# A four-layer graph network on one core: softmax transposes, the first quad's edge sums and the order of the first iteration are changed

## The chip, the cores and the metric

One core of one Trainium2 chip runs the whole network in one launch. The metric is device time in microseconds (us). TensorE (PE in the profile, PEld for its weight loads) multiplies, VectorE (DVE) and ScalarE (ACT) work on tiles, GpSimd (POOL) issues indirect transfers and some elementwise work, and SyncE (SP) issues plain transfers.

## The reference

Input x holds 128 batches of 128 nodes with 256 features, in fp32. Each of four layers computes `x = layernorm(x + g(x))`. The first g is graph attention over 512 edges with four heads:

```python
Xq = (H @ W_lin.T).reshape(bt, n, h, dh);  Xv = (H @ W_val.T).reshape(bt, n, h, dh)
e = einsum('behd,hd->beh', leaky_relu(Xq[:, src] + Xq[:, dst], 0.2), a)
e = e + log(A0[src, dst] + 1e-8)
attn = softmax of e over the edges that share src
Y = segment_sum(attn * Xv[:, dst], src) @ W_out.T
```

The second g is three graph convolutions with weighting adj*adj and widths 512, 1024 and 256, with relu after the first two. The third multiplies with the diagonal, upper and lower parts of adj and three weights, and adds a bias. The fourth normalises adj, applies it, and runs two linear layers, each with a batch norm over all batches and nodes.

## The kernel before, in words

The batches are worked on in 32 quads of four. A quad goes through these steps, each a function:

- `values_in` (L237, L239) transposes x; `values` (L251 to L253) makes the queries `qt` and the values `xv` of the first quads with one product per batch. Later quads use `queries`, a Strassen-like scheme of seven products (class `Seven`: p1, p5, p2, p6, p7, p4, p3; S1 to S4 are sums of the left blocks, `sums_a`, L180 to L183). `spill` (L260) writes the queries to DRAM.
- `gather` and `gather_last` (L329, on POOL's queue) fetch for 128 edges at a time the query rows of src and add those of dst. The edges are sorted by src; `perm` is the permutation as a 0/1 matrix, and `sorted_columns` (L998) makes the sorted index columns by products with it. An edge list of 512 has NE = 4 chunks, and a quad R = 16 rows (four batches, four heads).
- `score` (L344 to L349) computes e for one chunk, in `es`; the last chunk adds the log weights.
- `softmax_parts` is a generator, so that the caller decides where each part stands: four transposes of 128x16 to 16x128 (L356), a running maximum forward (L358) and backward (L361), subtract (L364), Exp (L365), a running sum forward (L367) and a running maximum backward (L369).
- `attention` (L379 to L383) transposes numerator and denominator back in eight pieces of 16x128 and divides; `scatter` (L389 on POOL, then L392 on SP) writes the attention into a dense matrix in DRAM and loads it; `by_row` (L402) reorders it.
- `aggregate` (L416) applies it to the values, `stage_a` (L430, L433, norms L105 to L120) ends layer 1.
- Layer 2: `mix1` (L441), `first` (L455) or `first_seven` (L280), `mix2` (L498), `late_sums` (L509, L510), `second` (L535, fourteen block products, with callbacks `between[i]` after product i), `third` (L616, a generator that yields after each quarter), `third_mix` (L629), `third_norm` (POOL's bias add is L640).
- Layer 3 is `stage_e` (L652, L657, L666; a generator). Layer 4 starts with `stage_f` (L697) and `hidden` (L726, L739), and a last phase after all quads ends it.

The order on every engine is that of the program (`manual_schedule`), and each engine runs its queue in order. In `iteration(k)` five quads are at work at once: k-1 in layers 3 and 4, k in layer 2, k+1 from aggregation to layer 2's first part, k+2 in scores and softmax, k+3 in queries and gather. `start()` sorts the edges, prepares matrices made from adj, and brings quads 0 to 3 as far as iteration 0 needs them. `iteration_0()` is written out by hand. In it, third runs whole, then aggregation and `stage_a` of quad 1, all of `stage_e(0)`, and layer 2's first part of quad 1.

In `start()` quad 0 is spilled and gathered like the others, the loads of `w1_sb` and the later weights are issued after `scatter(0)`, and quad 3's `values` stand after `stage_a(0)`.

Of the kernel before, what the change touches and what calls it, by code (L numbers as in the profile page):

```python
# [8 lines left out]
F32 = mybir.dt.float32  # L9
# [12 lines left out]
DROP = -1e30  # L22


@with_exitstack
def gnn_stack(ctx: ExitStack, tc: tile.TileContext, x, adj, w_qv_t, a, w_out_t, src, dst,
# [18 lines left out]
    P = 128  # L45
# [82 lines left out]
    with ExitStack() as phase:  # L128
        cst = phase.enter_context(tc.tile_pool(name="cst", bufs=1))

        class Quad:
            pass
# [91 lines left out]

        def temp(name):
            return wk.tile([P, 512], F32, tag="t", name=name, bufs=6)
# [15 lines left out]
        def values(k, i, copy=None, queue=None):  # L242
# [3 lines left out]
            if i == 0:  # L246
                s.qt = wk.tile([P, QB, D], F32, tag="xb", name=f"qt{k}", bufs=1)
                s.xv = ws.tile([P, QB, D], F32, tag="xv", name=f"xv{k}", bufs=3)
# [5 lines left out]
            if i == QB - 1:  # L254
                spill(k, queue)

        def spill(k, queue=None):
            s = quads[k]
            s.qd = q_dram[k % 4]
            (queue or nc.sync).dma_start(s.qd, s.qt.rearrange("p b d -> p (b d)"))  # L260
# [48 lines left out]
        def gather(k, z=None, chunks=range(NE - 1)):  # L309


            s = quads[k]
            s.z = z or {}
            for c in chunks:
                if c not in s.z:
                    s.z[c] = z_buffer(k, c)
            jobs = [(t, c) for t in range(2) for c in chunks]
            if k == 0:
                jobs = [(0, 0), (0, 1), (1, 0), (0, 2), (1, 1), (0, 3), (1, 2), (1, 3)]
            for t, c in jobs:  # L320
                gather_one(k, t, c)
# [11 lines left out]
        def gather_last(k):  # L333
            quads[k].z[NE - 1] = z_buffer(k, NE - 1)
            for t in range(2):
                gather_one(k, t, NE - 1)

        def score(k, c):

            s = quads[k]  # L340
            if c == 0:
                s.es = ws.tile([P, NE, R], F32, tag="es", name=f"es{k}", bufs=1)
# [5 lines left out]
            if c == NE - 1:  # L348
                nc.vector.tensor_add(s.es, s.es, log_col.unsqueeze(2).to_broadcast([P, NE, R]))  # L349

        def softmax_parts(k):

            s = quads[k]
            pe = ps("pe")
            for c in range(NE):
                nc.tensor.transpose(pe[:R, c * P:(c + 1) * P], s.es[:, c, :], ident)  # L356
            f = wk.tile([R, E], F32, tag="f", name="f", bufs=1)
            nc.vector.tensor_tensor_scan(f, reset_f, pe[:R, :], initial=0.0, op0=ALU.add, op1=ALU.max)  # L358
            yield
            m = wk.tile([R, E], F32, tag="m", name="m", bufs=1)  # L360
            nc.vector.tensor_tensor_scan(m[:, ::-1], reset_b[:, ::-1], f[:, ::-1], initial=0.0,  # L361
                                         op0=ALU.add, op1=ALU.max)
            yield
            nc.vector.tensor_sub(f, pe[:R, :], m)  # L364
# [4 lines left out]
            nc.vector.tensor_tensor_scan(m[:, ::-1], keep_b[:, ::-1], m[:, ::-1], initial=0.0,  # L369
                                         op0=ALU.mult, op1=ALU.max)  # L370
            s.ex, s.den = f, m

        def attention(k):

            s = quads[k]
            pa = ps("pat")[:, :2 * NE * R].rearrange("p (s c r) -> p s c r", s=2, c=NE)
            for i, t in ((0, s.ex), (1, s.den)):
                for c in range(NE):
                    nc.tensor.transpose(pa[:, i, c, :], t[:, c * P:(c + 1) * P], ident[:R, :R])  # L379
            rden = wk.tile([P, NE, R], F32, tag="rden", name="rden", bufs=1)  # L380
            nc.vector.reciprocal(rden, pa[:, 1])
            s.at = wk.tile([P, NE, R], F32, tag="at", name="at", bufs=1)
            nc.vector.tensor_mul(s.at, rden, pa[:, 0])  # L383

        def scatter(k):
            s = quads[k]
            ad = att_dram[k % 2]
            for c in range(NE):
                nc.gpsimd.indirect_dma_start(out=ad, out_offset=bass.IndirectOffsetOnAxis(ap=att_idx[:, c:c + 1], axis=0),  # L389
                                             in_=s.at[:, c, :], in_offset=None)  # L390
            s.ad = wk.tile([P, N * R], F32, tag="ad", name=f"ad{k}", bufs=1)
# [397 lines left out]
        def iteration(k):  # L789
# [6 lines left out]
            parts = quads[a].layer2 if a > 0 else iter(())  # L796
# [5 lines left out]
            for _ in parts:  # L802
                pass
            if has_c:
                between = {i: [] for i in range(14)}
                if has_e:
# [632 lines left out]
```

## Time and profile before

| what | us |
|---|---|
| runs: lowest, median, highest of 3 | 3214.33, 3216.5, 3216.66 |
| the profiled execution, by its own time | 3216.53 |
| its span, first to last instruction | 3214.8 |
| PE busy | 3132.8 (97%) |
| DVE busy | 2143.9 (67%) |
| ACT busy | 1276.8 (40%) |
| POOL busy | 663.5 (21%) |

Instructions are grouped by line, engine and operand shapes, as `out<-in`. An fp32 product appears as two matmul records, a transpose as one. Records are pipelined: a record's own duration is longer than the distance from its start to the next start, and the distance is what a product costs. PEclk is the granted share of TensorE's full clock. A line of the waits gives the engine that waited, who released it, the time in all, how often, and the longest.

### The profile page before, as it was taken

The numbers are of one execution on the slowest core, as the hardware profiler recorded it, in microseconds if no ns is written. First come the engines' busy times: TensorE is split into PE (matmuls) and PEld (weight loads), VectorE is DVE, ScalarE is ACT, GpSimd is POOL, SyncE is SP. The second block draws the span as 40 slices with busy tenths as digits, with TensorE's granted clock in tenths as the row PEclk, the third lists the DMA queues.
The fourth block names the chain that finished last, engine by engine and source line by source line (L and its number), as shares of the span: only waits on it lengthen the run. The fifth ranks groups of instructions, "written<-read, shape, count | busy, mean of one in ns | idle before, by whom it ended". The sixth has DMA issues, their size and how long they took to land. (4 is left out here: it accounts for less than half of the span.)

```text
span 3214.8 us, 41204 instructions
## 1 busy us (share of the span) xinstructions
PE 3132.8 (97%) x15884; PEld 2596.4 (81%) x15884; DVE 2143.9 (67%) x4200; ACT 1276.8 (40%) x2229; POOL 663.5 (21%) x541
## 2 busy tenths in 40 slices
PE   6999999999999999999999999999999999999997
PEld 3788888888888888888888888888888888874444
DVE  6666666666666666666666667666666666437878
ACT  2343333333333333333333333343333333326668
POOL 4202222122111111222112221111222211002135
PEclk7999999999999999999999999999999999999999
DMA  7613333333333223333333333223333321005557
GB/s 216 182 47 99 106 99 105 91 101 106 99 92 101 87 78 97 106 99 106 99 92 106 106 86 106 88 80 90 106 100 105 100 85 53 21 27 183 177 191 274
DMA packets 118756, 344.86 MB, mean 107 GB/s; under 512 B 15008, under 2 KB 51744, under 8 KB 110240
## 3 DMA queue, kind: packets, MB, share of 16 engines
q0 software_dynamic: 45552, 151.55, 19.3%
q1 hardware_dynamic: 70960, 188.71, 16.2%
q8 instruction: 126, 2.06, 0.3%
q10 hardware_dynamic: 2048, 1.97, 0.2%
q14 instruction: 70, 0.57, 0.1%
HBM read 256.20 MB, written 85.98 MB: 106 GB/s over the span
## 5 line engine op out<-in xcount | busy, mean ns | idle before, releaser
L535 PE MATMUL ph<-m,w 128*128 128x256 f32 x2048 | 464.3, 380 | 0.0
L616 PE MATMUL p<-w,h 128*128 128x256 f32 x2048 | 462.3, 379 | 0.0
L616 PEld LDWEIGHTS p<-w,h 128*128 128x128 f32 x2048 | 389.6, 190 | 65.6 <-issue 7.6
L535 PEld LDWEIGHTS ph<-m,w 128*128 128x128 f32 x2048 | 388.0, 191 | 51.0
L329 POOL DMA_INDIRECT zs<-qd,src_idx x123 | 119.5, 972 | 1390.1 <-DVE z L739 769.7
L535 PE MATMUL ph<-m,w_s 128*128 128x256 f32 x1536 | 352.5, 379 | 0.0
L666 PE MATMUL po<-l2w,ms 128*128 128x256 f32 x1536 | 348.3, 380 | 1.3 <-DVE ms L658 1.3
L535 PEld LDWEIGHTS ph<-m,w_s 128*128 128x128 f32 x1536 | 292.2, 190 | 39.3
L666 PEld LDWEIGHTS po<-l2w,ms 128*128 128x128 f32 x1536 | 285.3, 191 | 36.0 <-DVE ms L658 1.5
L329 POOL DMA_INDIRECT zs<-qd,dst_idx x123 | 211.2, 1717 | 254.9 <-DMA zs<-qd,src_idx 242.1
L112 ACT ACTIVATE ln_sd<-ln_mv,eps 128x2 f32<-128x2 f32 x192 | 56.3, 293 | 498.8 <-DVE ln_mv L107 498.8
L389 POOL DMA_INDIRECT attd<-at,att_idx x128 | 126.1, 986 | 358.9 <-DMA attd<-at,att_idx 253.5
L548 DVE TENSOR_TENSOR h<-ph,u 128x512 f32<-128x512 f32 x128 | 88.1, 689 | 167.8 <-PE ph L535 114.5
L542 ACT COPY u<-ph 128x512 f32<-128x512 f32 x128 | 74.9, 585 | 244.3 <-PE ph L535 244.3
L346 DVE TENSOR_TENSOR zs<-zs,a_bc 128x1024 f32<-128x1024 f32 x123 | 150.7, 1225 | 4.2
L347 DVE TENSOR_REDUCE es<-zs 128x16 f32<-128x1024 f32 x123 | 150.1, 1220 | 4.2
L344 DVE SCALAR_TENSOR_TENSOR zs<-zs 128x1024 f32<-128x1024 f32 x123 | 149.6, 1216 | 2.1 <-DMA zs<-qd,dst_idx 2.1
L120 DVE TENSOR_SCALAR xr<-xr,ln_mv,ln_rs 128x256 f32<-128x256 f32 x384 | 143.6, 416 | 7.0
L654 ACT COPY ms<-pm 128x512 f32<-128x512 f32 x128 | 71.1, 579 | 194.4 <-PE pm L652 191.0
L105 DVE BATCH_NORM_STATS2 ln_st<-xr 128x6 f32<-128x256 f32 x384 | 144.2, 417 | 5.5
L477 DVE TENSOR_TENSOR h<-z,adc 128x512 f32<-128x512 f32 x62 | 41.9, 675 | 153.8 <-ACT adc L471 153.8
L640 POOL TENSOR_TENSOR xb<-xr,bias 128x512 f32<-128x512 f32 x64 | 81.6, 1275 | 293.6 <-DVE xr L120 155.6
(298 smaller groups left out, 5713.1 us busy)
## 6 DMA issues: line engine op xcount, KB each, us to landing
ad<-attd SPq DMA_DIRECT2D x32, 1024.0 KB, 4.7
zd<-z SPq DMA_DIRECT2D x31, 1024.0 KB, 7.3
zl<-zd SPq DMA_DIRECT2D x62, 512.0 KB, 3.5
xr<-in_x_dram SPq DMA_DIRECT2D x32, 512.0 KB, 5.8
x3d<-xr SPq DMA_DIRECT2D x32, 512.0 KB, 2.8
x3l<-x3d SPq DMA_DIRECT2D x32, 512.0 KB, 4.9
out_dram<-x3l POOLq DMA_DIRECT2D x31, 512.0 KB, 5.3
qd<-qt SPq DMA_DIRECT2D x30, 512.0 KB, 2.6
```

Of the source, the lines that this page charges most:

```text
L105: nc.vector.bn_stats(st[:, i, :], r[:, i, :])
L120: nc.vector.tensor_scalar(r[:, i, :], r[:, i, :], mv[:, i, 0:1], rs[:, i:i + 1], op0=ALU.subtract, op1=ALU.mult)
L329: nc.gpsimd.indirect_dma_start(out=s.z[c], out_offset=None, in_=s.qd, in_offset=bass.IndirectOffsetOnAxis(ap=idx[:, c:c + 1], axis=0), com ...
L344: nc.vector.scalar_tensor_tensor(z, z, SLOPE, z, op0=ALU.mult, op1=ALU.max)
L346: nc.vector.tensor_mul(z3, z3, a_bc.unsqueeze(1).to_broadcast([P, QB, D]))
L347: nc.vector.reduce_sum(s.es[:, c, :], z.rearrange("p (r d) -> p r d", d=DH), axis=AX.X)
L389: nc.gpsimd.indirect_dma_start(out=ad, out_offset=bass.IndirectOffsetOnAxis(ap=att_idx[:, c:c + 1], axis=0), in_=s.at[:, c, :], in_offset= ...
L535: nc.tensor.matmul(bank[g][:, i].rearrange("p b n -> p (b n)"), wa[:, c, f:f + P], s.m2[:, blk_b, c].rearrange("p b n -> p (b n)"), start= ...
L548: nc.vector.tensor_add(block(g, row, col), bank[g], kept_[g])
L616: nc.tensor.matmul(p3[:, t * D:(t + 1) * D], s.h2[f // 2][:, f % 2, j + t, :], w3_sb[:, f, :], start=(f == 0), stop=(f == K2 - 1))
L640: nc.gpsimd.tensor_add(s.xb[:, j:j + 2, :], xj, bias.unsqueeze(1).to_broadcast([P, 2, D]))
L666: nc.tensor.matmul(po[:, i % 2, :], mss[i][:, t, dc, :], l2w[:, t, dc, :], start=(n3 == 0), stop=(n3 == 3 * DC - 1))
```

## The change

1. `scores` and `pair` are two new fixed tiles, set to zero once. `scores` keeps a chunk's 16 columns in a block of 32, so that one 128x128 transpose turns all four chunks; four ScalarE copies bring the blocks to `pair[:16]`. The denominator goes to `pair[32:48]`, so that `attention` transposes four pieces of 48x128 instead of eight of 16x128.
2. The parts of the softmax stand earlier in the loop: the transpose after product 11 of `second`, both maxima after product 12, the subtract ahead of `queries`, Exp after q's first product.
3. Quad 0 is neither spilled nor gathered. Its edge sums are products of a one-hot matrix (ones at src and dst) with the queries, in the order of the list; its scores take the weights in `score`, and products with `perm` sort them while they are transposed. The loads of all weights are issued before the first products. Quad 1's gathers wait for the end of this, and its dst gathers alternate with quad 0's scatters. `second_sums` and quad 3's queries stand ahead of quad 0's `by_row`.
4. `iteration_0` follows the loop's order: third's quarters lie between the steps of quads 1 and 2, and all but the first part of `stage_e(0)` goes to iteration 1's beginning. Quad 1's softmax crosses from `start` into `second(0)`.

```diff
+        scores = ctile([P, NE, GAP], "scores", pool=cst)
+        pair = ctile([GAP + R, E], "pair", pool=cst)
+        nc.vector.memset(scores, 0.0)
+        nc.vector.memset(pair, 0.0)
...
+        def ends_sum(k, h, onehot):
+            s = quads[k]
+            for c in range(NE):
+                pz = ps("pz")
+                nc.tensor.matmul(pz, onehot[:, c * P:(c + 1) * P], s.qt[:, 2 * h:2 * h + 2, :], start=True, stop=True)
+                nc.scalar.copy(s.z[c][:, h * 512:(h + 1) * 512], pz)
+        def sorted_scores(k, perm, chunks=range(NE)):
...
+            for c in chunks:
+                nc.tensor.matmul(s.pe[:R, :], s.es[:, c, :], perm[:, c, :], start=(c == 0), stop=(c == NE - 1))
...
-        def score(k, c):
+        def score(k, c, weight=None):
...
+            if weight is not None:
+                nc.vector.tensor_scalar(s.es[:, c, :], s.es[:, c, :], weight[:, c:c + 1], None, op0=ALU.add)
+            elif c == NE - 1:
...
         def softmax_parts(k):
...
-            for c in range(NE):
-                nc.tensor.transpose(pe[:R, c * P:(c + 1) * P], s.es[:, c, :], ident)
...
+            f, m = pair[:R], wk.tile([R, E], F32, tag="m", name="m", bufs=1)
+            rows = s.pe[:R, :] if s.pe is not None else None
+            if rows is None:
+                rows = f
+                pe = ps("pe")[:, :P]
+                nc.tensor.transpose(pe, scores.rearrange("p c r -> p (c r)"), ident)
+                for c in range(NE):
+                    nc.scalar.copy(f[:, c * P:(c + 1) * P], pe[c * GAP:c * GAP + R, :])
...
         def attention(k):
...
-            for i, t in ((0, s.ex), (1, s.den)):
-                for c in range(NE):
-                    nc.tensor.transpose(pa[:, i, c, :], t[:, c * P:(c + 1) * P], ident[:R, :R])
+            for c in range(NE):
+                nc.tensor.transpose(pa[:, c, :], pair[:, c * P:(c + 1) * P], ident[:GAP + R, :GAP + R])
...
+                between[11].append(lambda: next(steps, None))
+                between[12] += [lambda: next(steps, None)] * 2
...
         def iteration_0():
...
-            between[1] = [lambda: attention(1), lambda: scatter(1)]
-            between[2] = [lambda: score(2, 0), lambda: gather_last(2)]
+            between[0] = [lambda: score(2, 0), lambda: gather_last(2, range(1))]
+            between[1] = [lambda: next(quads[1].steps), lambda: next(quads[1].steps, None)]
+            between[3] = [lambda: attention(1), lambda: scatter(1), lambda: gather_last(2, range(1, 2))]
...
+            rest = third(0, 0)
+            next(rest)
+            first_seven.blocks = weight_blocks(w1_sb, w1_s)
+            for j in range(QB):
+                by_row(1, j, nc.vector.tensor_copy if j % 2 else None)
+            next(rest)
+            aggregate(1)
             score(2, NE - 1)
-            first_seven.blocks = weight_blocks(w1_sb, w1_s)
+            next(rest)
+            stage_a(1)
+            for _ in rest:
+                pass
+            steps = softmax_parts(2)
+            for _ in range(5):
+                next(steps)
+            third_mix(0, 0)
+            rest = third(0, 2)
+            next(rest)
+            third_norm(0, 0)
+            mix1(1, 0)
+            mix1(1, 2)
+            next(rest)
+            w = first_seven(1)
+            for _ in steps:
+                pass
+            run(w.p1, w.p5, w.p2)
+            next(rest)
+            attention(2)
+            scatter(2)
+            w.p6()
+            next(rest, None)
+            w.p7()
+            third_mix(0, 2)
+            w.p4()
+            w.p3()
+            third_norm(0, 2)
+            quads[0].layer2 = stage_e(0)
+            next(quads[0].layer2)
+            for i in range(QB):
+                mix2(1, i)
...
+            onehot = scratch("onehot")
...
+            for h in range(2):
+                for i in range(2):
+                    values(0, 2 * h + i, nc.scalar.copy,
+                           xv=borrowed[:, N * R:N * R + QB * D].rearrange("p (b d) -> p b d", d=D))
+                ends_sum(0, h, onehot)
...
+            sorted_scores(0, perm, range(NE - 1))
+            sorted_columns((0, 1))
+            sorted_scores(0, perm, (NE - 1,))
+            sorted_columns((2, 3))
...
+                gather_one(1, 0, c)
...
             attention(0)
...
+            scatter(0, lambda c: gather_one(1, 1, c))
```

`...` stands for what is left out.

## Prediction

> **What bounds it now.** I read the page first, for the engine that is full, and where.
>
> ```profile
> span 3214.8 us, 41204 instructions
> ...
> PE   6999999999999999999999999999999999999997
> ...
> PEclk7999999999999999999999999999999999999999
> ```
>
> TensorE is full in all but the first and last slices. The stage table, cut where layer 2's first product of each quad starts (timeline: 110.1, 201.0, 288.7, then every 87.47 us), shows where it is not:
>
> ```profile
> core 0: us, PE busy (x) PEld busy (x) DVE busy (x) ACT busy (x) POOL busy (x), PEclk, DMA share, GB/s
> 0.00:52.10 52.10, 32.91 (x120) 19.22 (x120) 30.77 (x66) 10.76 (x24) 27.92 (x28) 0.82 0.83 241
> 52.10:110.10 58.00, 43.77 (x182) 28.09 (x183) 40.13 (x64) 20.12 (x39) 14.64 (x14) 0.79 0.80 235
> 110.10:201.00 90.90, 80.01 (x399) 68.73 (x398) 55.36 (x108) 28.30 (x47) 21.33 (x18) 0.91 0.29 81
> 201.00:288.70 87.70, 87.56 (x470) 76.48 (x469) 61.20 (x113) 33.27 (x56) 17.57 (x14) 1.00 0.33 91
> ```
>
> From 201 us each iteration is pure TensorE at full clock: a record taken out there shortens the span by its own spacing, no more. Before 201 us there is slack of another kind: start and iteration 0 hold idle time and work at half clock. TensorE's waits, first from 0 to 112 us, then from 110 to 202, name it:
>
> ```profile
> PE pe L356 <- DVE es L349: 10.8, 1, 10.8
> PE py L416 <- ACT adc L402: 8.0, 1, 8.0
> ...
> PE pcol L998 <- DVE ends L1035: 3.1, 1, 3.1
> ```
>
> ```profile
> PE po L430 <- ACT yt L419: 3.9, 1, 3.9
> PE pat L379 <- ACT f L365: 2.7, 1, 2.7
> PE pm L498 <- ACT h L478: 2.2, 1, 2.2
> PE pat L379 <- DVE m L369: 2.1, 1, 2.1
> ```
>
> Quad 0's scores, then its scattered attention, set the start; in iteration 0, steps written one after another do.
>
> **Term 1, the loop's transposes.** TensorE's timeline in one iteration, scores and then attention:
>
> ```profile
> 663.63 1.95 PE L697 MATMUL pa<-ahat_t,xr 128*128 128x128 f32 x16
> 665.42 0.60 PE L356 MATMUL pe<-ident,es 128*16 128x128 f32 x4
> 665.86 1.03 PE L280 MATMUL y<-wqv,xt 128*128 128x256 f32 x4
> ```
>
> ```profile
> 689.75 0.81 PE L616 MATMUL p<-w,h 128*128 128x256 f32 x3
> 690.49 0.41 PE L379 MATMUL pat<-ident,f 16*128 16x16 f32 x4
> 690.76 0.40 PE L379 MATMUL pat<-ident,m 16*128 16x16 f32 x4
> 691.09 2.05 PE L441 MATMUL pm<-wt_t,xr 128*128 128x128 f32 x16
> ```
>
> Start to start, the four score transposes take 665.86-665.42 = 0.44, 0.11 each. The wide 128x128 ones of line 237 also stand 0.11 apart (eight from 659.30 to 660.18). One for four saves 0.33. The eight attention transposes take 0.60, plus 0.09 lost on entry (three records of 0.216 from 689.75 would end at 690.40): 0.69. Two narrow ones stand 0.06 apart, and the last, before L441, takes 0.14. Four of 48x128 cost 0.09+3x0.06+0.14 = 0.41 if they keep that spacing, 0.56 if they take the wide one's 0.11; no row has this shape. I take 0.43, near the narrow end, because both kinds load 128 columns and 48 moving columns stream in 0.04 at line 535's rate (256 in 0.216). Saving 0.26 (0.13 to 0.28), with the scores 0.59 (0.46 to 0.61). Twenty-nine iterations carry it (quads 3 to 31): 17 us, 13.3 to 17.7.
>
> The Trainium skill's page "TensorE: Matmul & The Clock Gate", section "Back-to-back issue gap", speaks against that size: it gives N/2.4+2.5 ns, 56 ns for 128 columns, where this trace has 109 in fp32. By it the score transposes would save 0.17 and the term be 12 us; the measured spacing decides.
>
> What the loop gains elsewhere must stay hidden. Four ScalarE copies of 16x128 replace the scans' read of PSUM: rows nearest are 0.20 (L1099, 128x1) and 0.37 (L503, 128x256), so 0.8 to 1.5 us, at 659.9 after a relu; ScalarE is then idle until 662.11, which covers them. Uncovered, they would cost up to 29x1.5 = 44. The transpose now stands inside `second`, after its twelfth product, where line 237 starts at 659.30; behind it wait all TensorE work. It needs L349, which ends at 657.81: 1.49 to spare. VectorE gets two scans (2.45) ahead of the total at 663.83, and is idle for the 2.44 before that. The total and the following subtract (0.41, as L180 reads SBUF) delay S1, due by about 666.2, from 664.85 to about 665.5. Exp and its table (1.28+0.63) move ahead of the copy at 669.5, which must be done before q's product at 671.0 overwrites its bank; they end near 669.1. So no new wait: 0.
>
> **Term 2, the start.** Before, quad 0 goes through DRAM: sort (18.9), spill, eight gathers, scores done at 51.9 with weights, scan at 53.2, attention at 61.3, four scatters (61.55, 63.98, 67.53, 69.90), load issued 72.04, landed 76.9, layer 2 at 110.1.
>
> After: two more memsets lie ahead of VectorE's wait for the edge list at 6.9, free. The one-hot adds 0.48+0.69 (as L978, L971) and waits for row dst (issued 2.49, 6.1 to land: 8.6), so VectorE's ranks and pair weights shift by about 1.9, but no longer stand idle from 13.1 to 18.9 for sorted columns: done at 22.4. On TensorE, eight 128x512 products (16 records x 0.43 = 6.9 us, as line 251) stand between the query products; ScalarE's eight copies (0.58) end at 24.4, and Ln with its table (1.28+0.20) stands behind them: 25.9. That wait is new; VectorE waits 3.5 us for it. Four scores at 3.65 (40.68 to 44.33) plus a 0.2 add, and the 1.6 of keep and reset: 26.6+15.4+1.6 = 43.6. Sorting the scores is eight records, of which the last two and sixteen of sorted columns (0.11 to 0.17) follow: scan at about 45, 8 us earlier. Softmax and attention take what they took, plus four index copies and quad 2's first query product on TensorE: scatter at 54.5, 7 earlier.
>
> Here part is given back. The four scatters alternate with quad 1's add-gathers on POOL's queue, and four gathers are ahead. A scatter step took 2.4 (later ones) to 3.55 (with gathers in flight): I take 3.5, load issued at 67.5 (64.7 to 70), landed 72.4. SP must issue the weight loads, 10.7 MB with x, before quad 1's spill: at 300 GB/s (the stage from 10 to 20 us moved 311) about 36 us plus the bias rows that took 6.6 at 97.3: free by 45, gathers start 48.8. Late by what exceeds 4.
>
> VectorE between has 2.6 of adjacency work, `second_sums` 4.7 (99.60 to 104.3 before), two scores: 72. TensorE puts the other seven query products of quads 2 and 3 (1.72 each) ahead of quad 0's aggregation, the last three behind a transpose that waits for a score until 67.2, their first 3.4 us at half clock; ScalarE puts their copies ahead of `by_row`, which starts at 75. Aggregation ends at 78.3, the second norm at 85.9 (83.1 to 91.8 before), mix1 at 86.8. Then, from `first` (before: 96.1 to 110.1 = 14.0, with `second_sums` and Exp in the way), 11.7: eight records 3.4, slow clock 1.5, three `mix2`, two `first`, last `mix2` 6.8. Layer 2 starts at 98.5: 11.5 gained. With everything serial and 3 us late per hand-over it is 106 (gain 4); with scatters at 2.4 and full clock, 93 (gain 17).
>
> Idle also costs clock: stages 40 to 50 and 70 to 80 are granted 0.50, where a 128x512 record takes 0.86. The same page, section "The HAM clock gate", says that after about 3.4 us idle the clock halves until 3.4 us of work has passed. Three such waits would cost 3x1.7 = 5 us by it; above stand 2 to 2.5 for each of two.
>
> **Term 3, iteration 0.** It takes 90.9; its records at full spacing (112 of L535, 64 of L616, 48 of L666, ...) make 73, so 18 are lost: 10.9 in the waits above, 7 in slow clock. The last parts of `stage_e(0)` (12.5 us) go to iteration 1's head, still ahead of the next mark, so nothing leaves. After, third's quarters (1.73 each) lie between aggregation, stage A, mix1 and the seven products. Losses left: attention(1) waits for scores(2,0) and two scans, 2.4; `by_row(1)` (scatter at 113, load at 123, landed 128) 0.7; third's copy 0.6; Exp, Sqrt and the mix copies in ScalarE's order before the first product, 2.0. With transposes 0.6 cheaper, 77.5 to 78: 13 gained (8 to 16). Quad 1's Exp and scans now cross into `second`, and scatter(1) moves from its second product to after its fourth, already counted. On SP, the spill of quad 3 and the load of quad 4 follow the attention load, long before gather(3) at 123; the store of quad 0's layer-2 output falls behind the load of attention(2), and only the last phase reads it. On POOL, gather(3) and scatter(2) stand ahead of the two bias adds, whose sum is first read about 167, and they end by 164.
>
> **Sum.** The profiled execution took 3216.53 beside its span of 3214.8, and the runs' median is 3216.5: no correction. 3216.5 - 17 - 11.5 - 13 = 3175; bounds 13.3+4+8 = 25 and 17.7+17+16 = 51: 3166 to 3191.
>
> **Rivals.** (a) The start gains nothing: SP's loads or the alternating queue hold quad 1 and the scatter until 72; for it, l2w's issue alone held SP 17.36 us at 74.8. Then 3216.5-17-8 = 3191.5. (b) Head free of loss: start 17, iteration 16, 3166; against it, VectorE is nearly gapless from 7 to 90. (c) Slower: VectorE's hand-over in the loop. Transposes, four copies, two scans, total, subtract, S1 form one new chain with 0.7 spare, and q's second product stands behind it in TensorE's order. Every us beyond 0.7 costs 29; it decides at 0.7+41.5/29 = 2.1 us late. At 3 us late it gives 3216.5-41.5+67 = 3242. Against: the row times above and a trace in which all iterations are alike. (d) The 48-row transposes cost the wide price: 3179, within the forecast.
>
> Measurement tells about 0.2% (6.4 us) from no change. Forecast 0.72, (a) 0.14, (b) 0.08, (c) 0.05, no visible change through half of (c) 0.01. Range 3162 to 3197. Faster 0.94, same 0.01, slower 0.05.
>
> **To check.** The mark spacing falls from 87.47 to 86.9; pat takes 0.43; no TensorE wait on scores or S1 after 190 us; first scatter near 54.5, load near 67.5, marks at 98.5 and 176. A spacing of 87.5 or more refutes term 1; a first mark past 106, term 2.

## The result, and the profile after

The changed kernel takes 3188.35 us (median of 4 runs, 3187.98 to 3188.80) against 3215.41 of the kernel before on the same chip (4 runs, 3209.44 to 3216.66): a ratio of 0.992, 95% interval 0.9902 to 0.9937. That is 27 us of the 41.5 that were forecast: the direction was right, the size was not. The profiled execution took 3188.38 with a span of 3186.6, to be compared with 3214.8 before.

From the page of the changed kernel, its span, TensorE's busy tenths and its granted clock:

```profile
span 3186.6 us, 40910 instructions
...
PE   7899999999999999999999999999999999999997
...
PEclk8899999999999999999999999999999999999999
```

It is still a kernel that TensorE fills, with slack at both ends only. The start of layer 2's first product (now L562) stands at 108.61, 190.97 and 277.89 us, then every 86.92. The stage table is cut at the events of quad 0: first scatter, attention load issued, aggregation begun, first mark, second mark, third mark.

```profile
core 0: us, PE busy (x) PEld busy (x) DVE busy (x) ACT busy (x) POOL busy (x), PEclk, DMA share, GB/s
0.00:56.70 56.70, 47.97 (x132) 23.81 (x133) 39.98 (x82) 19.19 (x38) 12.20 (x18) 0.88 0.67 227
56.70:73.94 17.24, 14.12 (x39) 6.34 (x37) 14.28 (x21) 6.33 (x16) 12.05 (x10) 0.90 0.77 160
73.94:83.23 9.29, 0.45 (x2) 0.00 (x0) 1.11 (x3) 1.75 (x4) 0.00 (x1) 0.73 0.96 259
83.23:108.61 25.38, 22.42 (x113) 16.66 (x114) 16.36 (x29) 7.44 (x16) 8.13 (x6) 0.83 0.59 154
108.61:190.97 82.36, 76.88 (x387) 64.96 (x386) 61.34 (x112) 29.16 (x51) 21.90 (x18) 0.96 0.30 78
190.97:277.89 86.92, 86.92 (x462) 75.85 (x461) 59.04 (x114) 33.87 (x60) 17.09 (x14) 1.00 0.35 98
```

The third row is the one to see: from 73.94 to 83.23 the engines nearly stand still (TensorE works 0.45 us of 9.29, VectorE 1.11, ScalarE 1.75), while the DMA engines are 96% busy. Quad 0's attention load is on its way. TensorE's waits, from 0 to 112 us and from 98 to 200, say the same, and name what is left in iteration 0:

```profile
PE py L443 <- ACT adc L429: 8.8, 1, 8.8
```

```profile
PE pat L404 <- DVE pair L396: 3.2, 2, 2.4
PE po L656 <- ACT s L648: 1.9, 1, 1.9
```

The marks divide the 28.2 us between the spans. Start: 110.12 to 108.61, 1.5 gained (11.5 forecast). Iteration 0: 90.85 to 82.36, 8.5 gained (13). Second mark to last, 2613.5 to 2597.3: 16.2 gained (17). Behind the last mark 2.0, not forecast; in the runs below that stretch lasts 396.9 to 400.3 with no pattern, so these 2 us are scatter.

The loop term can be read off TensorE's timeline, scores first, attention second:

```profile
645.65 0.81 PE L562 MATMUL ph<-m,w_s 128*128 128x256 f32 x3
646.29 0.27 PE L381 MATMUL pe<-ident,scores 128*128 128x128 f32 x1
646.40 0.38 PE L245 MATMUL pt<-ident,xg 128*128 128x128 f32 x2
...
676.20 1.03 PE L643 MATMUL p<-w,h 128*128 128x256 f32 x4
677.15 0.44 PE L404 MATMUL pat<-ident,pair 48*128 48x48 f32 x4
677.53 0.38 PE L468 MATMUL pm<-wt_t,xr 128*128 128x128 f32 x1
```

The score transpose costs 646.40-646.29 = 0.11. The four 48x128 pieces cost 677.53-677.15 = 0.38, and 0.09 on entry (four records of 0.216 from 676.20 would end at 677.06): 0.47. From 201 us to the tail no wait of TensorE for scores or S1 appears.

The start can be read off POOL's timeline, scatters (L414) and quad 1's add-gathers (L331, dst_idx):

```profile
56.70 0.99 POOL L414 DMA_INDIRECT attd<-at,att_idx  x1 [0.31 <-DVE src_row L1119]
57.99 1.64 POOL L331 DMA_INDIRECT z<-qd,dst_idx  x1 [0.30 <-issue]
62.16 1.11 POOL L414 DMA_INDIRECT attd<-at,att_idx  x1 [2.53 <-DMA attd<-at,att_idx]
63.57 1.57 POOL L331 DMA_INDIRECT zs<-qd,dst_idx  x1 [0.30 <-issue]
65.45 1.37 POOL L414 DMA_INDIRECT attd<-at,att_idx  x1 [0.30 <-issue]
67.13 1.56 POOL L331 DMA_INDIRECT zs<-qd,dst_idx  x1 [0.30 <-issue]
69.83 1.69 POOL L414 DMA_INDIRECT attd<-at,att_idx  x1 [1.14 <-DMA attd<-at,att_idx]
71.82 1.56 POOL L331 DMA_INDIRECT z<-qd,dst_idx  x1 [0.30 <-issue]
```

A step takes (69.83-56.70)/3 = 4.4, where 3.5 was taken. The load is issued at 73.94 and lands 8.2 later. In the first two microseconds behind its issue, 74 to 76, the queue table of the DMA engines shows POOL's queue (q0) alone, at the full share of the 16 engines; the load's own queue (q1), which carries what SyncE issues, moves nothing:

```profile
q0 software_dynamic: 83, 0.34, 103.7%
```

Before, in the same place of quad 0's load (74 to 77, load issued at 72.04, landed in 4.9), it was q1 that had the engines:

```profile
q1 hardware_dynamic: 143, 0.94, 77.8%
q0 software_dynamic: 51, 0.21, 17.1%
```

### The profile page after: what moved, and what is told of

It is laid out like the page before. It is cut to its first block, busy times and chain, and to the rows that moved or that the text cites. A ratio compares the mean times of both kernels' runs of the same rounds, so it can differ in the third digit from the quotient of the medians.

```text
span 3186.6 us, 40910 instructions
## 1 busy us (share of the span) xinstructions
PE 3119.4 (98%) x15651; PEld 2574.5 (81%) x15651; DVE 2162.4 (68%) x4209; ACT 1311.9 (41%) x2359; POOL 649.2 (20%) x533
## 5 line engine op out<-in xcount | busy, mean ns | idle before, releaser
L562 PE MATMUL ph<-m,w 128*128 128x256 f32 x2048 | 463.0, 379 | 0.0
L562 PEld LDWEIGHTS ph<-m,w 128*128 128x128 f32 x2048 | 386.8, 190 | 51.4
L331 POOL DMA_INDIRECT zs<-qd,src_idx x122 | 118.3, 970 | 1407.8 <-DMA qd<-qt 829.0
L562 PE MATMUL ph<-m,w_s 128*128 128x256 f32 x1536 | 354.4, 380 | 0.0
L562 PEld LDWEIGHTS ph<-m,w_s 128*128 128x128 f32 x1536 | 292.9, 191 | 40.2
L331 POOL DMA_INDIRECT zs<-qd,dst_idx x122 | 207.6, 1701 | 244.1 <-DMA zs<-qd,src_idx 236.2
L414 POOL DMA_INDIRECT attd<-at,att_idx x128 | 127.8, 998 | 300.6 <-DMA attd<-at,att_idx 239.3
L367 DVE TENSOR_REDUCE scores<-zs 128x16 f32<-128x1024 f32 x125 | 152.5, 1220 | 4.3
```

The costliest lines, as they stand in the source:

```text
L331: nc.gpsimd.indirect_dma_start(out=s.z[c], out_offset=None, in_=s.qd, in_offset=bass.IndirectOffsetOnAxis(ap=idx[:, c:c + 1], axis=0), com ...
L367: nc.vector.reduce_sum(s.es[:, c, :], z.rearrange("p (r d) -> p r d", d=DH), axis=AX.X)
L562: nc.tensor.matmul(bank[g][:, i].rearrange("p b n -> p (b n)"), wa[:, c, f:f + P], s.m2[:, blk_b, c].rearrange("p b n -> p (b n)"), start= ...
```

## The experiments

Times are medians of 4 runs (four_transposes: 3). Since one program's runs spread over 1 to 8 us, the verdicts rest on the marks of the profiled execution. The marks scatter too: in the six runs that leave the start as it is (four_transposes but for three records), the first mark lies between 107.29 and 111.27 (108.61 in the changed kernel) and the first scatter between 56.7 and 57.7; in the three that leave iteration 0 as it is (no_add and the early_gathers), its spacing lies between 82.6 and 83.3 (82.36). In the diffs, `...` and comments stand for lines that are left out.

**What holds quad 0 in the start.** no_add:

```diff
-            scatter(0, lambda c: gather_one(1, 1, c))
+            scatter(0)
```

> Leaves out quad 1's four add-gathers in the start (quad 1's scores then come from the source rows alone), so that the four scatters of quad 0 stand next to each other on POOL. Theory A, the add-gathers between the scatters, and the last one ahead of the attention load on the DMA engines, cost quad 0 its gain: after the first scatter at 56.7 the steps fall from 4.4 us to 3.5, 2.4, 2.4, the load is issued at 56.7+3.5+2.4+2.4+2.4 = 67.4 (73.9 in the changed kernel) and lands in 4.9 us instead of 8.2, at 72.3 (82.1); with the 26.5 us from there to layer 2's first product, the first mark comes at 98.8 (108.6), and the time falls to about 3188.4 - 9.8 = 3178.6. Rival B, a scatter costs over 4 us here whoever stands beside it: steps stay at 4 us, load at 73 or later, mark at 105 or later, time 3185 or more. Rival E, the load comes early but TensorE's queue of query products (until 74.4 us) or VectorE is the next bound: load landed at 72, mark still at 103 or later, time about 3183.

Measured: 3184.13 us, the profiled execution 3180.87 with a span of 3179.1; load issued at 69.02, landed at 74.98, first mark at 99.19. POOL's timeline:

```profile
57.37 0.99 POOL L414 DMA_INDIRECT attd<-at,att_idx  x1 [0.49 <-DVE src_row L1118]
61.99 0.97 POOL L414 DMA_INDIRECT attd<-at,att_idx  x1 [3.62 <-DMA attd<-at,att_idx]
64.39 0.96 POOL L414 DMA_INDIRECT attd<-at,att_idx  x1 [1.43 <-DMA attd<-at,att_idx]
66.76 1.10 POOL L414 DMA_INDIRECT attd<-at,att_idx  x1 [1.41 <-DMA attd<-at,att_idx]
```

Alone, a scatter takes 2.4; only the first, behind the source gathers, takes 4.6. The mark comes 9.4 us sooner (9.8 expected): theory A. By_row begins 7.1 sooner; the other 2.3 are a shorter way from the aggregation to the mark (23.10 instead of 25.38), since TensorE waited 1.7 us instead of 8.8 ahead of it and less of the work behind ran at half clock. So the add-gathers cost quad 0, by both ways, nearly all that the start should have won. The median fell by 4.2 only; of the profiled execution's 9.4, 1.7 were lost again behind the last mark, where nothing was changed.

early_gathers and early_gathers_2 keep all the work and move the gathers ahead:

```diff
+            # sorted src and dst alone; early_gathers: behind src_row, early_gathers_2: behind quad 1's queries
+            for c in range(NE):
+                for i in range(NE):
+                    nc.tensor.matmul(pe01[:, c, :], perm[:, i, c * P:(c + 1) * P], ends[:, :2, i],
+                                     start=(i == 0), stop=(i == NE - 1))
...
+            nc.vector.tensor_copy(src_idx, pe01[:, :, 0])
+            nc.vector.tensor_copy(dst_idx, pe01[:, :, 1])
...
+            # ahead of sorted_scores: all gathers of quad 1
-            scatter(0, lambda c: gather_one(1, 1, c))
+            scatter(0)
```

> Moves, leaves nothing out: the sorted columns of source and target alone are made by 16 products of two columns right after src_row (27 us), so quad 1's eight gathers start when its spill has landed (about 42 us) instead of at 50.8, and the four scatters stand next to each other. Theory A: the gathers are over by about 55, the scatters start at 56.7 and step by 2.4, load issued at 56.7+4x2.4 = 66.3, landed at 71.2; TensorE's query products end at 74.4, so the aggregation starts at 73.5 to 74.5 and the first mark comes at 98 to 100; time 3178 to 3180. Rival B, the scatter itself is dear: steps of 4 us, load at 73, mark at 105 or later. Rival F, the early gathers only move the collision, onto the sort and the scores of quad 0 or onto the loads of the weights: first scatter after 58, mark at 104 or later.

Measured: 3192.80 us, slower than the changed kernel; first mark at 112.00. Quad 0's attention was ready at 55.7, but its scatter stood behind the last pair of gathers on POOL:

```profile
57.78 0.98 POOL L331 DMA_INDIRECT z<-qd,src_idx  x1 [0.30 <-issue]
66.58 1.53 POOL L331 DMA_INDIRECT z<-qd,dst_idx  x1 [7.82 <-DMA z<-qd,src_idx]
68.42 1.02 POOL L414 DMA_INDIRECT attd<-at,att_idx  x1 [0.30 <-DVE zs L364]
```

This is rival F in another form: the gathers were still landing, and POOL's order turned that into 12.8 us. The steps behind it were 4.7, 2.4 and 2.4, so A holds here too.

> As early_gathers, leaving nothing out, but the products for the sorted source and target stand behind quad 1's query products (in TensorE's idle time from 35.6 us) and all eight gathers ahead of quad 0's scatters in the order source 0 to 3, target 0 to 3. In early_gathers the products ran ahead of quad 1's queries, pushed its spill from 36.1 to 42.8, and a gather whose source landed late kept POOL from the scatter until 68.4. Theory A, it is the add-gathers in between that cost quad 0: gathers from 42, the last one issued by about 55, first scatter at 56 to 58, steps 2.4 after the first one, load issued at 66 to 68.5, landed by 73, TensorE's query products end at 74, first mark at 98 to 100, time 3178 to 3181. Rival F, eight gathers of 0.5 MB need 16 us or more of the DMA engines wherever they stand, so they run past 58 and push scatter and load again: first scatter after 59 or load after 71, mark at 104 or later, time 3184 or more.

Measured: 3182.69 us; load issued at 69.87, landed at 75.82, first mark at 102.76, 5.9 sooner. Between A and F: the later steps are short and the load lands in 6.0, but the first scatter, issued behind eight gathers, takes 6.7 us until the next can go:

```profile
52.78 1.53 POOL L331 DMA_INDIRECT z<-qd,dst_idx  x1 [0.30 <-issue]
55.47 1.02 POOL L414 DMA_INDIRECT attd<-at,att_idx  x1 [1.16 <-DVE src_row L1128]
62.17 1.14 POOL L414 DMA_INDIRECT attd<-at,att_idx  x1 [5.68 <-DMA attd<-at,att_idx]
```

**What half clock costs.** warm and warm_2 put products that nobody reads into TensorE's waits:

```diff
+        def warm(n):
+            pw = ps("pw")
+            for _ in range(n):
+                nc.tensor.matmul(pw, ident, wqv[:, 0, :], start=True, stop=True)
...
+            warm(9)   # ahead of by_row(0); 3 and 2 in the head, 2 ahead of attention(1); in warm twice these or more
```

> Adds 32 products of the identity with 512 columns, whose result nobody reads, in four of TensorE's waits: 6 and 3 around quad 0's third and fourth score (37.5 to 45 us), 18 ahead of the aggregation of quad 0 (74.4 to 83.2), 5 ahead of attention(1) (115.6 to 118.0). Theory C, it is these waits that leave TensorE at half clock behind them: the head's 16 sorted columns and quad 2's transposes and products go at the full rate, first scatter at 55 instead of 56.7; the 26.5 us from the landed attention load to the first mark become 23.5; the spacing from the first to the second mark falls from 82.4 to 80.6; in all 3 to 6 us, time 3182 to 3185. Rival D, the clock costs nothing, since VectorE and ScalarE set the pace in those stretches: marks within 0.7 us of the changed kernel's, time 3187.5 to 3189.5; or later, by what the added products themselves take.

Measured: 3193.81 us, slower. The expectation counted one record to a product, and an fp32 product leaves two: the 18 products took 15.6 us and ended 6.5 after the load had landed. But from the aggregation's first product (91.18) to the first mark (114.18) it was 23.0 us instead of 25.4.

> As warm, with the added products counted rightly: each leaves two records of 0.43 us in the trace, so warm had twice the work that was meant and ran past the waits. Now 3 and 2 products around quad 0's third and fourth score, 9 ahead of its aggregation, 2 ahead of attention(1). Theory C, half clock behind a wait costs what it doubles: first scatter at 55 to 56 instead of 56.7; from the aggregation's first product to the first mark 23.0 us (25.4 in the changed kernel, 23.0 in warm); spacing of the first to the second mark 80.6 instead of 82.4; time 3183 to 3185. Rival D, VectorE and ScalarE set the pace: 25 us and 82.2, time 3187.5 or more.

Measured: 3184.41 us; first scatter at 54.94 (1.8 sooner), aggregation to first mark 23.03, first mark at 104.00. Its stage table, from load to aggregation and from there to the mark, has 7.42 us of products, nearly all filler, in the first row and a granted clock of 0.93, where the changed kernel has 0.83, in the second:

```profile
72.38:80.97 8.59, 7.42 (x19) 3.00 (x17) 1.11 (x3) 1.49 (x4) 0.10 (x1) 1.00 0.97 268
80.97:104.00 23.03, 20.13 (x113) 14.54 (x114) 16.28 (x30) 7.43 (x16) 8.21 (x6) 0.93 0.69 174
```

Theory C in the start: half clock costs 2.4 us behind the load and 1.8 ahead of the scatter (the first scatter of the unchanged starts is never before 56.7, and the mark never before 107.29). In iteration 0 it failed: the spacing stayed at 82.55, with new waits of 2.0 at the seven products and 1.0 at by_row(1). Something else sets the pace there.

**Iteration 0.** old_iteration puts the old order back:

```diff
+            between[0] = [lambda: next(quads[1].steps), lambda: next(quads[1].steps, None)]
+            between[1] = [lambda: attention(1), lambda: scatter(1)]
...
+            # then the lines of before, stage_e(0) whole
```

> Undoes one part: iteration 0 in its old order (third of all four quarters ahead of stage A, the whole of stage_e(0) inside), with the last two scans of quad 1 ahead of its attention; start and loop as changed. Theory G, the order made the gain of iteration 0: the spacing from the first to the second mark goes from 82.4 back to about 90.3 (90.9 of before less 0.6 of cheaper transposes), time 3188.4 + 8 = 3196. Rival H, what the start leaves behind (quad 1's softmax done sooner, the weights loaded, quad 3's values spilled) made it: spacing 84 to 86, time 3190 to 3192.

Measured: 3199.05 us; spacing 91.48, and 2.4 more in the next one (89.30). The order carries the gain, as theory G says. The size is not clean: TensorE's waits for the two attentions are 9.0 us here and were 4.8 before, so 9.1 is an upper end and about 5 the lower one.

scan_first, attention_first, mix_first and iteration_fixed then move steps of the new order:

```diff
-            between[0] = [lambda: score(2, 0), lambda: gather_last(2, range(1))]
-            between[1] = [lambda: next(quads[1].steps), lambda: next(quads[1].steps, None)]
+            between[0] = [lambda: next(quads[1].steps), lambda: next(quads[1].steps, None)]
+            between[1] = [lambda: score(2, 0), lambda: gather_last(2, range(1))]       # scan_first
...
+            between[3] = [lambda: attention(1), lambda: scatter(1), lambda: score(2, 0), lambda: gather_last(2, range(1))]   # attention_first
+            for c, i in ((1, 5), (2, 7)):       # attention_first
```

> One move in iteration 0: quad 1's last two scans go ahead of score(2,0) on VectorE. Theory C: attention(1)'s wait for them (2.4 us) goes, and with it the half clock behind it (16 records at double time, 1.8 us lost): the spacing from the first to the second mark falls from 82.4 to 78.2, time 3184. Rival K, only the wait is won and the clock halves anyway: 80. Rival L, score(2,0) now holds up the additions that free layer 2's PSUM banks (the first of them at 118.8 instead of 117.9), and TensorE waits there: 81 or more, time 3187 or more.

Measured: 3191.98 us, spacing 86.26: slower. TensorE's waits between its first two marks:

```profile
PE py L443 <- ACT adc L429: 3.9, 1, 3.9
```

The wait for the attention is gone, and the half clock behind it. But the scatter stayed at 122.7, because the division that makes its data stands behind score(2,1) in VectorE's order (its end at 121.7), and TensorE waited for by_row instead, with half clock behind that wait. L's numbers fit but not its cause: TensorE waited 0.3 for layer 2's banks.

> One move in iteration 0: quad 1's last two scans and its attention go ahead of all of quad 2's scores on VectorE (score(2,0) behind the attention, the other two two products later). In scan_first the wait of attention(1) went away but the scatter stayed at 122.7, since the reciprocal and product that make its data stood behind score(2,1), and TensorE waited 3.9 us for by_row(1) instead. Theory P, iteration 0 is bound by that chain on VectorE, attention to scatter to load to by_row(1): first scatter of quad 1 falls from 123.3 to about 117.5 (14.7 to 9 us after the first mark), load at about 127.5, no wait of TensorE for attention(1) or by_row(1), and the spacing of the first two marks falls from 82.4 to 78 to 79, time 3184. Rival Q, behind it stands the next chain of equal length (norms, scans, Exp, copies of mix1 in ScalarE's order, which took 19.5 us from aggregation to the seven products in two runs): spacing 80 to 81.5, with a wait of 2 us at the seven products. Rival L, the additions of layer 2 wait behind the scores: 82 or more.

Measured: 3187.95 us, spacing 81.07: rival Q. The scatter comes at 117.58, 8.6 behind the mark, and neither attention(1) nor by_row(1) is waited for; the longest waits left are

```profile
PE y L288 <- ACT mx L471: 2.0, 1, 2.0
PE po L656 <- ACT s L648: 1.9, 1, 1.9
```

The aggregation begins 28.30 us behind the mark instead of 32.39, so 4.1 are won. From there to the first of the seven products it is 19.5 us here, 19.5 in the changed kernel, 19.6 in warm_2 and in early_gathers_2, though TensorE's records there are worth only 15.4 (iteration_fixed, below): in this order the copies of mix1 stand behind Exp on ScalarE, and Exp behind the norms and scans on VectorE. Behind it 2.8 are lost again:

```profile
156.78 1.55 PE L288 MATMUL y<-w,mx 128*128 128x256 f32 x4 [2.02 <-ACT mx L471]
158.93 2.04 PE L288 MATMUL z<-w,adc 128*128 128x256 f32 x4 [0.59 <-DVE adc L181]
160.76 1.91 PE L288 MATMUL x<-w,mx 128*128 128x256 f32 x4
```

From 156.78 to 164.20 the granted clock is 0.54, and the four records of z and the four of x take 1.8 and 1.7 us instead of 0.9 each. In the changed kernel the wait in this place was 0.3 and the clock stayed full.

```diff
             steps = softmax_parts(2)
-            for _ in range(5):
-                next(steps)
-            third_mix(0, 0)
+            next(steps)
             rest = third(0, 2)
             next(rest)
+            third_mix(0, 0)
+            mix1(1, 0)
+            mix1(1, 2)
             third_norm(0, 0)
...
+            # scans and Exp between first_seven and its parts; attention(2) behind w.p7 (mix_first) or w.p4 (iteration_fixed)
```

> One reordering in iteration 0: after quad 2's score transpose, the first quarter of third's second half goes ahead of third_mix(0,0), the two mix1 of quad 1 go ahead of quad 2's scans and Exp, and attention(2) goes behind the seven products' seventh. Theory M: the copy of third's first half waited behind the square root of stage A in ScalarE's order (TensorE idle 1.9 us, then half clock, 1.5 lost), and attention(2) behind two scans (0.8): the spacing of the first two marks falls from 82.4 to 78 to 79, time 3184 to 3185. Rival N, VectorE's norms, scans and sums of this stretch are one chain, and the wait goes to the seven products or to attention(2): 81.5 or more, time 3187.5 or more.

Measured: 3191.85 us, spacing 85.22: rival N. The wait at third_mix fell from 1.9 to 0.2, and came back double (the 2.4 is attention(1), as in the changed kernel):

```profile
PE y L288 <- ACT adc L498: 3.9, 1, 3.9
PE pat L404 <- DVE pair L396: 2.4, 1, 2.4
```

The copy of a part of the seven products stood behind Exp in ScalarE's order, and Exp waited for the scans.

> attention_first, and in the second half of iteration 0 the copies of mix1 and of the seven products' parts ahead of quad 2's Exp on ScalarE, its scans between the seven products' sums and totals on VectorE, attention(2) behind the fourth product. Theory M, in mix_first it was the copy of a part behind Exp that took the gain back (3.9 us): now spacing 75 to 77, time 3180 to 3182. Rival N, VectorE's chain of norms, sums and scans is as long in any order: 79 or more, time 3185 or more.

Measured: 3185.66 us, spacing 80.33: rival N again, by its number. With Exp behind that copy the wait is 2.4, and the attentions wait 2.1. Six orders of this stretch gave 80.3 to 91.5, and none reached the 78 of the forecast. Cut at TensorE's aggregation and at the first of the seven products (combined is the last run below), the iterations are

| run | mark to aggregation | to the seven products | to the next mark | last two together |
|---|---|---|---|---|
| changed kernel | 32.39 | 19.49 | 30.48 | 49.97 |
| scan_first | 32.84 | 22.29 | 31.13 | 53.42 |
| attention_first | 28.30 | 19.48 | 33.29 | 52.77 |
| mix_first | 32.39 | 15.58 | 37.26 | 52.84 |
| iteration_fixed | 28.30 | 15.71 | 36.32 | 52.03 |
| combined | 28.30 | 15.85 | 35.47 | 51.32 |

So 19.5 us is no fixed length: with the copies of mix1 ahead of Exp the stretch falls to 15.7. What is won there is lost behind it, and none of these orders got from the aggregation to the next mark in less than the changed kernel's 50.0. All of the gain, 4.1 us, lies ahead of the aggregation. Why the rest stays above 50 is not shown: N's one chain on VectorE was not tested alone, and VectorE is busy only 39.2 of iteration_fixed's 52.0 us.

**The loop.**

```diff
-                nc.tensor.transpose(pe, scores.rearrange("p c r -> p (c r)"), ident)
+                for c in range(NE):
+                    nc.tensor.transpose(pe[:R, c * P:(c + 1) * P], scores[:, c, :R], ident)
```

> Undoes one part in all iterations: the scores are transposed again by four transposes of 16 columns in place of one of 128. Theory T1 of the prediction: each of the three costs its spacing of 0.11, so the marks of the steady iterations stand 86.92+0.33 = 87.25 apart, and the time is 3188.4+29x0.33 = 3198. Rival, the transposes hide in the wait for something else: 86.9 to 87.0 and 3188 to 3190.

Measured: 3201.71 us (span 3197.8). The steady spacing is 87.25 to the digit, one iteration by the stage table:

```profile
280.38:367.63 87.25, 87.25 (x465) 76.24 (x464) 59.14 (x114) 33.62 (x60) 17.19 (x14) 1.00 0.34 97
```

Second mark to last grew by 9.5 us (9.6 for 29 times 0.33): theory T1. The span grew by 11.2, since the first mark came 2.7 later (111.27) while iteration 0 and the tail were 0.5 shorter each; those three are scatter of one execution.

**The moves that helped, together.** combined is iteration_fixed and early_gathers_2, with the last pair of quad 1's gathers behind quad 0's scatters:

```diff
-                for c in range(NE):
-                    gather_one(1, t, c)
+                for c in range(NE - 1):
+                    gather_one(1, t, c)
...
             scatter(0)
+            for t in range(2):
+                gather_one(1, t, NE - 1)
```

> The moves that helped, together, leaving nothing out: the sorted source and target by early products as in early_gathers_2, but only three of quad 1's four pairs of gathers ahead of quad 0's scatters and the fourth behind them; and iteration_fixed. Theory A and F together (six gathers end about 55, the four scatters are then alone): first scatter at 55.5, the next at 59 to 60 instead of 62.2, then steps of 2.5, load issued at 67 and landed by 73, first mark at 97 to 100 (102.8 in early_gathers_2, 108.6 in the changed kernel); spacing to the second mark 80.3 to 82; time 3175 to 3179. Rival F alone, DMA work in front of the load is what counts, and the fourth pair now stands in front of it: load landed at 75 or later, first mark at 102 or later, time 3181 or more.

Measured: 3177.82 us (3173.71 to 3181.99), ratio to before 0.9889, interval 0.9871 to 0.9906. Its runs lie below all runs of both kernels. Its stage table, cut at the load's issue, the aggregation and the marks:

```profile
66.63:75.31 8.68, 5.20 (x14) 1.99 (x12) 4.60 (x6) 3.70 (x10) 2.67 (x4) 1.00 0.88 284
75.31:100.01 24.70, 21.82 (x113) 15.80 (x114) 16.40 (x30) 7.45 (x16) 7.78 (x6) 0.86 0.70 177
100.01:179.63 79.62, 74.78 (x388) 63.33 (x386) 62.38 (x112) 29.27 (x51) 21.59 (x18) 0.98 0.31 81
```

First mark at 100.01, second at 179.63 (190.97 in the changed kernel). The load, issued at 66.63, still took 7.5 to land; the fourth source gather was issued ahead of it, at 65.79. It landed between the two forecasts (73 and 75), so in part rival F holds.

## Why the prediction was right or wrong

**The sum.** 3175 us were forecast and 3188.35 measured. That lies inside the stated 3162 to 3197, but by the width of the range and not by the mechanism: the loop gave what was forecast, the start 1.5 of 11.5 us and iteration 0 8.5 of 13. By the prediction's own sign, a first mark past 106, term 2 is refuted (108.61), and rival (a) with 3191.5 came closer than the forecast. The 2.0 us behind the last mark were luck.

**The bound** was right: outside start and iteration 0 a record of TensorE taken out shortens the span by its spacing, and nothing else moved. Rival (c), a wait of the loop on VectorE, did not come; TensorE shows no such wait.

**Term 1** was right: 87.47 to 86.92, 0.55 an iteration (0.59 forecast). The score transposes saved 0.33 as worked out, and four_transposes gave just that back. The 48x128 pieces were the part that was off: 0.47 with their entry instead of 0.43, between the two ends. The 56 ns for 128 columns that the prediction took from the Trainium skill's page "TensorE: Matmul & The Clock Gate", section "Back-to-back issue gap", would have made the spacing of the score transposes half of what they cost. The page calls this formula the gap of an isolated product and gives about 81 ns for a stream of loads and products; the measured 0.109 us is above both, and it was the one to use.

**Term 2** was wrong, and its failed step is the one that took 3.5 us for a scatter between add-gathers and 4.9 for the load. VectorE's part had come out nearly to the tenth: Ln at 25.9 (25.9 forecast), quad 0's scores done at 43.9 (43.6). Then the first scatter came at 56.7 instead of 54.5: the last score transposes and columns ran at half clock, as did quad 2's products ahead of the attention (warm_2 gets 1.8 of the 2.2 back). The four steps to the load's issue took 17.2 instead of 13.0, the load 8.2 instead of 4.9. By_row began at 82.1 instead of 75, and the way from there to the mark took 26.5 instead of 23.5, of which warm_2 gives 2.4 to the clock. (The prediction says that it holds 2 to 2.5 us for each of two such waits; its sum holds 1.7 and 1.5.)

The 3.5 came from a misread row. The step of 3.55 in the kernel before was taken for one "with gathers in flight", but from 63.98 to 67.53 there it was a spill of 0.5 MB, issued by SP at 64.48, that moved:

```profile
q1 hardware_dynamic: 144, 0.52, 36.9%
q0 software_dynamic: 32, 0.01, 1.1%
```

So no row that the steps were priced by had a gather in flight; in the changed kernel there were four ahead of the scatters and four more between them. The prediction also let the load start when SP issued it, and did not ask what was already queued on the DMA engines: the load's queue moved nothing until about 76.5. In the six other runs with this start the load took 7.5 to 8.8; in the three with no gather just ahead of it, no_add, early_gathers and early_gathers_2, 5.6 to 6.0. In kind that is rival (a), the alternating queue, which had 0.14 and the price of 3191.5, though the first scatter was not held until 72 but went at 56.7; its other half, SP's loads, did not happen (SP was free at 34.9, quad 1's spill out at 36.1). What the one-hot sums and the early weight loads are worth by themselves is not shown; no run takes one of them back.

The Trainium skill's page "DMA: Bandwidth & Descriptors", section "Issuing engines are not separate DMA queues", says that transfers issued from different engines end up on the same 16 DMA engines and interleave. The traces agree that they share the engines, and mostly that they interleave: from 74 to 77 before, q1 had 77.8% and q0 17.1%, and in combined, from 68 to 71, q1 52.0% and q0 44.9%. But in the changed kernel the load's queue moved nothing for 2.5 us behind its issue while the gather had the engines; before, and in no_add, its first packet came after 1 us. Whether it matters that this gather adds, or only that its packets were there first, no run tells.

**Term 3** was mis-sized by 4.6, and its failed step is the list of losses (5.7 us), which priced a wait as idle time alone. The waits themselves measured 5.4 in all, attention(1) with 2.4 as forecast; the half clock behind them, part of the 7 us of slow clock in the kernel before, stood at nothing. TensorE's timeline around attention(1):

```profile
113.80 1.89 PE L562 MATMUL ph<-m,w_s 128*128 128x256 f32 x8
118.05 0.42 PE L404 MATMUL pat<-ident,pair 48*128 48x48 f32 x4 [2.37 <-DVE pair L396]
118.40 3.98 PE L562 MATMUL ph<-m,w_s 128*128 128x256 f32 x10
```

Eight records behind it start 0.427 apart instead of 0.216: 1.8 lost. Behind third's copy (a wait of 1.9 where 0.6 was forecast) another 1.5. About 1.5 more are not traced. But the experiments show that a list of TensorE's losses does not add up to a gain either: take a wait and its half clock away (attention_first, 4.1 us) and 1.3 are won, because TensorE then waits further on, for the copies of mix1, and loses 2.8 there. Where a wait goes when it is taken away, the prediction never asked. By old_iteration the order is worth 5 to 9 of the 8.5.

The same skill's page "TensorE: Matmul & The Clock Gate", section "The HAM clock gate", puts the drop to half clock behind about 3.4 us of idling. Here waits of 2.4 and 1.9 us were each followed by 3.4 us of it, and attention_first's waits of 2.0 and 0.6 by 6.8. The length of a wait does not decide it: 2.4 us ahead of the same attention(1) in early_gathers_2, and 1.9 ahead of the same copy in attention_first, were followed by none (16 records in 3.56 us, eight in 1.73). The measurement decides, so a wait of 2 us has to be priced at 2 to 4.8.

## What to carry to other kernels

Price a transfer by what is already queued on the DMA engines when it is issued, not by its own length: a gather of 0.5 MB put between or ahead of small transfers on the critical path cost 0.8 to 2.2 us each time (the changed kernel against no_add). Before a row is used as a price "with gathers in flight", look in the queue table whether any were. Price a wait of an engine whose clock depends on its load with the slow stretch that may follow. And in a stretch written by hand, ask of each wait that is taken away which wait comes next: taking waits away won 1.3 of 4.1 us once and made the end later twice.

## What was not expected of the hardware

An accumulating gather held all 16 DMA engines at a share of 99% to 106% for the 2.5 us in which a plain load of 1 MB, already issued, moved nothing. A scatter of 128 pieces takes 2.4 us from issue to issue with free DMA engines, 3.2 to 6.7 with gathers in flight. And TensorE's clock halved for 3.4 us (eight records of 0.427) behind a wait of only 1.9 us, and not at all behind one of 1.9 in another run.
